# A bound on the scatters under way in a GNN layer: each tied scatter waits for the one three ahead of it

## The chip, the cores and the metric

The kernel runs on one core of a Trainium2 chip, in one launch. The metric is the device time of one execution in microseconds (us). Beside the timed runs there is one profiled execution, from which all durations below are taken.

## The reference, cut to what matters

A graph has 6250 nodes with 128 features each and 100,000 edges, which are sorted by their destination (`dst`) and have their sources (`src`) in no order. Each edge makes a message from its two nodes' features and its own 128 features; the messages are summed by source node.

```python
row, col = src, dst
h = jnp.concatenate([x[row], x[col], edge_attr], axis=-1) @ W + b
h = layernorm(h) * gamma + beta
msg = relu(h)
out = segment_sum(msg, row, num_segments=6250)
return layernorm(x + out)
```

## The kernel before, in words

**Tiles.** The edges are cut into 782 tiles of 128. Four tiles make a *slot* `q` (196 slots, `PT = 4`). The nodes are split into 50 blocks by `src % 50`, which are worked on as 25 pairs of blocks.

**First half of an edge's way (by slot).** For each slot, `edges` (L602) multiplies the edge features `eT` with the third part of the weights (L611) and adds the destination node's part, picked out of a small window of a table by a 0/1 matrix (L615). `evict` (L619) lets ScalarE copy the PSUM bank into one of eight buffers `hs_all[q % 8]` (L623), with the source's local number beside it (L624). The eviction of slot `q + 8` therefore needs the buffer of slot `q`. From there each tile is *scattered*: `scatters` (L630) issues one indirect DMA on the queue of POOL (GpSimd) for each tile (L641), 128 rows of 528 bytes, to the rows of a table in DRAM, `sorted_d[s]`, that DVE has worked out (`place_i`). So there are 782 scatters. After them the rows of each pair of blocks lie together.

**Second half (by pair of blocks).** The slots are in six splits (`SPLITS`, of 168, 168, 168, 120, 80 and 78 tiles, that is 42, 42, 42, 30, 20 and 19.5 slots). A split's table can be read when all its scatters have landed. `load_pair` (L711, DMA at L715, on SP's queue) loads a pair's rows into `hl`; six steps later `ones` (L730) lets DVE build a 0/1 matrix `ohe` from it (L733), and after that come the turned matrix (L745, L749), the source node's part (L755, L772), the norm (L781, L784, L790, L796), the sum by node (L805) and the addition to `acc` (L810). The last split's rows are loaded in `Unit.load` (L831, DVE's matrix at L838), after the last slot.

**The order.** PE, DVE, ScalarE and SP run in an order written out by hand (`tc.manual_schedule`, L973). POOL is not in that list: where its instructions stand is decided by the framework's scheduler, from what each depends on. The loop over slots (L1118) does a slot's edge work and, in between, steps of the pairs' work; a table of due times (`due`, L1095) says that the pairs of split `s` start `LAG = 5` slots after the split's last slot.

**What a scatter waits for.** Up to slot 12 and in slot 195 the scatters are *untied*: they wait for their data, their rows' numbers and a semaphore of the DMA queue. Between them they are *tied* (`TIE`, L627; `scatters(..., True)`, L1144): in each slot the scatters of the slot before are issued, and each of them waits, too, for one of that slot's matmuls, so that they are spread over the slot (L647). Eight semaphores are used in turn for the scatters' landing, and a scatter waits for the landing of the one eight ahead, which had the same semaphore. Scatters of one split do not wait for each other's rows (`declare_no_dep`, L648).

Of the kernel before, what the change touches and what calls it, by code (L numbers as in the profile page):

```python
# [84 lines left out]
def fast_path(ctx, tc, io, bad_d, found):  # L85
# [3 lines left out]
    nc = tc.nc  # L89
# [6 lines left out]
    written = mybir.DependencyInfo(mybir.DependencyClass.Sync, mybir.DependencyReason.DATA)  # L96
# [528 lines left out]
        waiting.extend((s, q, j) for j in range(m))  # L625

    TIE = (12, 195)  # L627
    waiting = []

    def scatters(n, tied):  # L630

        total, seen, at = sum(c for _, c in done), 0, []
        for i, c in done:
            seen += c
            while len(at) < n and seen * n >= (len(at) + 1) * total:
                at.append(i)
        done.clear()
        for k, (s, q, j) in enumerate(waiting[:n]):
            t = q * PT + j
            parts = P if t < TILES - 1 else LAST  # L640
            i = nc.gpsimd.indirect_dma_start(  # L641
                out=sorted_d[s][:, :],
                out_offset=bass.IndirectOffsetOnAxis(ap=place_i[:parts, t:t + 1], axis=0),
                in_=hs_all[q % HS][:parts, j, :], in_offset=None,
            )
            if tied:
                tc.add_manual_dep(i.ins, at[k].name, written, reason="rows behind products")  # L647
            tc.declare_no_dep(i.ins, group=f"scatter{s}", reason="rows of different edges")  # L648
            tc.add_to_no_dep_group(f"scatter{s}", i.ins)
            if q < EARLY:  # L650
                tc.declare_no_dep(i.ins, group="clear", reason="see check_early")
                tc.add_to_no_dep_group("early", i.ins)
        del waiting[:n]
# [461 lines left out]
    for s, (n_tiles, _, _, _) in enumerate(SPLITS):  # L1115
        p0, p1 = first_tile[s] // PT, -(-first_tile[s + 1] // PT)
        slots = p1 - p0
        for i in range(slots):  # L1118
# [19 lines left out]
            if not TIE[0] <= q < TIE[1]:  # L1138
                scatters(len(waiting), False)
# [3 lines left out]
            if TIE[0] < q < TIE[1]:  # L1143
                scatters(len(waiting) - PT, True)  # L1144
# [115 lines left out]
@with_exitstack  # L1260
def gnn_resnorm_kernel(ctx, tc, io):
    nc = tc.nc
    keep = ctx.enter_context(tc.tile_pool(name="keep", bufs=1))
    bad_t = keep.tile([1, 1], I32, name="bad_t")
    with ExitStack() as inner:
        found = []
        fast_path(inner, tc, io, bad_t, found)
    with tc.If(found[0] > 0, preferred_fallthrough_block=True, label="general"):
        with ExitStack() as inner:
            general_path(inner, tc, io)  # L1270
# [233 lines left out]
```

## Time and profile before

| what | value |
|---|---|
| median of 3 runs | 1369.37 us (1368.53, 1369.37, 1379.85) |
| the profiled execution's own time | 1380.69 us, of which the span from the first to the last instruction is 1378.9 us |
| granted TensorE clock in it | 0.857 of full speed |
| first and last start of a scatter (L641) in it | 19.9 us and 1274.6 us |
| first and last start of a pair's load (L715) in it | 297.5 us and 1278.7 us |
| first and last start of a unit's load (L831) in it | 1281.7 us and 1344.5 us |

The engines are named PE (TensorE), DVE (VectorE), ACT (ScalarE), POOL (GpSimd) and SP (SyncE, which issues most of the DMAs). In the profile, a group's line has the source line, the engine, the operation, what it writes and reads, the number of instructions, then the busy time and the mean of one in ns, and after the bar the idle time of that engine just before them with what ended most of it. The time of a scatter on POOL is that in which POOL writes the transfer's descriptors; its data move afterwards, on the DMA engines, in the queue that the profile calls `q0 software_dynamic`. All other transfers of the kernel are in `q1 hardware_dynamic`. A scatter of a full tile is 32 packets in q0: 16 of data and 16 that raise its semaphore.

### The profile page before, as it was taken

What the parts mean: (1) busy time and instruction counts of PE and PEld (TensorE: products, weight loads), DVE (VectorE), ACT (ScalarE), POOL (GpSimd) and SP (SyncE); (2) the same over time, 40 slices, a digit from 0 to 9 for tenths busy, and PEclk for the clock granted to TensorE, in tenths of its full rate; (3) what the DMA queues carried; (4) which work ended last, traced back from release to release, by engine and by line L of the source; (5) the groups of instructions that cost most, each with busy time, mean ns of one, the idle gap of its engine ahead of it and who ended that gap; (6) DMA issues with size and microseconds to landing.
All of it is one profiled execution on the core that took longest, in us unless ns stands there. A gap on an engine that the chain in (4) does not pass through costs nothing. (4 is left out here: it accounts for less than half of the span.)

```text
span 1378.9 us, 27543 instructions
## 1 busy us (share of the span) xinstructions
PE 975.2 (71%) x8886; PEld 870.3 (63%) x8886; DVE 855.0 (62%) x2376; ACT 773.5 (56%) x3118; POOL 798.9 (58%) x835
## 2 busy tenths in 40 slices
PE   7457464345767676778777677778778787876895
PEld 5445453334666665777676667777778776765674
DVE  8573434524465656556575657678688867554797
ACT  4223232112555655564565557676778788665796
POOL 3656666666566665666565666566555555556054
PEclk9768687666888989878888899999999999988898
DMA  7758586455666655556656555665667655543332
GB/s 223 236 168 255 171 241 204 142 154 155 184 199 210 199 158 163 178 157 198 207 171 200 172 184 178 208 208 187 190 193 227 183 181 171 170 140 100 112 122 72
DMA packets 128052, 247.22 MB, mean 179 GB/s; under 512 B 47005, under 2 KB 61231, under 8 KB 127897
## 3 DMA queue, kind: packets, MB, share of 16 engines
q1 hardware_dynamic: 101924, 191.92, 46.8%
q0 software_dynamic: 25104, 53.05, 11.0%
q8 instruction: 71, 1.16, 0.4%
q14 instruction: 83, 0.68, 0.2%
q10 hardware_dynamic: 870, 0.40, 0.1%
HBM read 155.49 MB, written 89.80 MB: 178 GB/s over the span
## 5 line engine op out<-in xcount | busy, mean ns | idle before, releaser
L641 POOL DMA_INDIRECT sorted<-hs,place_i x782 | 760.4, 972 | 498.1 <-issue 210.6
L772 PE MATMUL sel<-xa,ohn 128*128 128x128 bf16 x2550 | 214.3, 232 | 174.9 <-issue 78.5
L781 ACT ACTIVATE sq<-sel 128x128 f32<-128x128 f32 x850 | 224.2, 280 | 158.9 <-PE sel L772 58.2
L772 PEld LDWEIGHTS <-ohn 128*128 128x128 bf16 x2550 | 174.8, 104 | 204.4 <-issue 174.7
L611 PE MATMUL hp<-w,eT 128*128 128x128 f32 x1564 | 258.3, 314 | 51.2 <-issue 37.9
L611 PEld LDWEIGHTS hp<-w,eT 128*128 128x128 f32 x1564 | 234.3, 225 | 83.2 <-issue 59.3
L805 PE MATMUL pa<-msg,ohe 128*128 128x130 f32 x1700 | 259.2, 308 | 24.1 <-issue 14.9
L623 ACT COPY hs<-hp 128x512 f32<-128x512 f32 x196 | 114.2, 583 | 288.7 <-issue 97.7
L805 PEld LDWEIGHTS pa<-msg,ohe 128*128 128x128 f32 x1700 | 236.4, 217 | 32.2 <-issue 19.0
L796 DVE SCALAR_TENSOR_TENSOR msg<-sel,rstd,cut 128x128 f32<-128x128 f32 x850 | 240.7, 345 | 8.0
L781 ACT ACTIVATION_READ_ACCUMULATOR sq<-sel 128x1 f32 x850 | 178.8, 210 | 0.0
L810 DVE TENSOR_TENSOR acc<-acc,pa 128x260 f32<-128x260 f32 x125 | 53.0, 424 | 201.0 <-PE pa L805 57.9
L733 DVE TENSOR_TENSOR ohe<-hl,beside 128x1024 f32<-128x1024 f32 (+2 forms) x125 | 131.4, 1052 | 23.3 <-PE sel L772 14.6
L749 ACT COPY ohn<-tr 128x1024 bf16<-128x1024 bf16 (+2 forms) x125 | 109.5, 876 | 37.9 <-PE pa L805 14.7
L755 ACT COPY sel<-hl 128x512 f32<-128x512 f32 (+1 forms) x225 | 127.9, 569 | 1.8 <-DVE msg L796 1.0
L599 DVE TENSOR_SCALAR ohd<-db,part_w 128x512 bf16<-128x512 bf16 x192 | 69.7, 363 | 72.1 <-remote 50.9
L615 PE MATMUL hp<-win,ohd 126*128 126x128 bf16 x782 | 88.5, 236 | 17.4 <-issue 15.4
L790 DVE RECIPROCAL rstd<-std 128x4 f32<-128x4 f32 (+1 forms) x225 | 38.6, 171 | 96.7 <-ACT std L784 45.2
L615 PEld LDWEIGHTS <-ohd 126*128 126x128 bf16 x782 | 69.0, 108 | 25.2 <-issue 20.9
L745 PE MATMUL tr<-ident_h,ohe 128*128 128x128 bf16 x850 | 75.5, 230 | 11.1 <-issue 9.4
L784 ACT ACTIVATE std<-ss,eps 128x4 f32<-128x4 f32 (+1 forms) x225 | 66.9, 297 | 7.3
L745 PEld LDWEIGHTS <-ohe 128*128 128x128 bf16 x850 | 57.7, 103 | 14.3 <-issue 14.2
(198 smaller groups left out, 1043.4 us busy)
## 6 DMA issues: line engine op xcount, KB each, us to landing
eT<-in_eT SPq DMA_DIRECT2D x96, 512.0 KB
hl<-sorted SPq DMA_DIRECT2D x75, 528.0 KB
db<-drel_d SPq DMA_DIRECT2D x96, 256.0 KB
sorted<-empty SPq DMA_DIRECT2D x100, 198.0 KB
hl<-sorted SPq DMA_DIRECT2D x50, 264.0 KB
sorted<-hs,place_i POOLq DMA_INDIRECT x782
hl<-sorted SPq DMA_DIRECT2D x25, 396.0 KB
sorted<-empty SPq DMA_DIRECT2D x50, 132.0 KB
```

Of the source, the lines that this page charges most:

```text
L611: pe(nc.tensor.matmul(hp[:, j, :], eT[:, at], w[:, 2, :], start=j == 0, stop=False, skip_group_check=True), 4)
L615: pe(nc.tensor.matmul(hp[:, j, :], oh[:3 * WN, at], win[:3 * WN, :], start=False, stop=j == m - 1, skip_group_check=True))
L623: nc.scalar.copy(hs[:, :m, 0:D], hp[:, :m, :])
L641: i = nc.gpsimd.indirect_dma_start(out=sorted_d[s][:, :], out_offset=bass.IndirectOffsetOnAxis(ap=place_i[:parts, t:t + 1], axis=0), in_=h ...
L733: nc.vector.tensor_tensor(self.ohe[:, :k, :], self.hl[:, :k, D:D + 1].to_broadcast([P, k, P]), row_bc(iota_p, k), op=ALU.is_equal)
L745: pe(nc.tensor.transpose(tr[:, j, :], half[:, j0 + j, 1::2], ident_h))
L749: nc.scalar.copy(self.ohn[:, :self.k, :], self.tr[:, :self.k, :])
L755: nc.scalar.copy(self.sel[g][:, :m, :], self.hl[:, j0:j0 + m, 0:D])
L772: pe(nc.tensor.matmul(sel[:, j, :], self.ohn[:, j0 + j, :], xa[:, b, i * D:(i + 1) * D], start=False, stop=j == m - 1 and i == 2, skip_gro ...
L781: nc.scalar.activation(sq[:, j, :], self.sel[g][:, j, :], AF.Square, accum_out=ss[:, j:j + 1])
L796: nc.vector.scalar_tensor_tensor(self.msg[:, j0 + j, 0:D], self.sel[g][:, j, :], rstd[:, j:j + 1], cut, op0=ALU.mult, op1=ALU.max)
L805: pe(nc.tensor.matmul(self.pa[:, h, :], self.ohe[:, j, :], self.msg[:, j, :], start=(j == h), stop=(j == k - 2 + h)), 4)
```

## The change

Ahead of each tied scatter the changed kernel records an instruction without work on POOL (`nop`), named `hold`, and makes it depend on the completion of the scatter that was recorded three before (`issued[-FLIGHT]`). Nothing else is changed. The scatter itself is not made dependent on `hold`.

```diff
     TIE = (12, 195)
-    waiting = []
+    FLIGHT, EVERY = 3, 1
+    waiting, issued = [], []
 
     def scatters(n, tied):
...
         for k, (s, q, j) in enumerate(waiting[:n]):
             t = q * PT + j
             parts = P if t < TILES - 1 else LAST
+            if tied and len(issued) % EVERY == 0:
+                hold = nc.gpsimd.nop()
+                tc.add_manual_dep(hold.ins, issued[-FLIGHT].name, written,
+                                  reason="so many scatters under way")
             i = nc.gpsimd.indirect_dma_start(
                 out=sorted_d[s][:, :],
                 out_offset=bass.IndirectOffsetOnAxis(ap=place_i[:parts, t:t + 1], axis=0),
                 in_=hs_all[q % HS][:parts, j, :], in_offset=None,
             )
+            issued.append(i.ins)
             if tied:
                 tc.add_manual_dep(i.ins, at[k].name, written, reason="rows behind products")
```

## The prediction, made before the changed kernel ran

> **What bounds the kernel now.** I read the page first, then POOL's waits, because the change adds waits there and nowhere else: in the built program PE, DVE, ACT and SP keep the same instructions, order and waits.
>
> ```profile
> span 1378.9 us, 27543 instructions
> PE 975.2 (71%) x8886; PEld 870.3 (63%) x8886; DVE 855.0 (62%) x2376; ACT 773.5 (56%) x3118; POOL 798.9 (58%) x835
> ...
> q1 hardware_dynamic: 101924, 191.92, 46.8%
> q0 software_dynamic: 25104, 53.05, 11.0%
> ...
> L641 POOL DMA_INDIRECT sorted<-hs,place_i x782 | 760.4, 972 | 498.1 <-issue 210.6
> ```
> ```profile
> POOL sorted L641 <- issue: 210.6, 535, 3.4
> POOL sorted L641 <- PE pa L805: 64.6, 53, 3.0
> ...
> POOL sorted L641 <- DMA sorted<-hs,place_i: 0.9, 3, 0.3
> ```
>
> No engine is full. The hand-written slots set the pace, and POOL follows: it waits for PE's products, and for the landing of an earlier scatter hardly ever (0.9 us in all, 3 times; that wait is for the one eight ahead). Behind a held scatter stand only further scatters on POOL's queue, so one wait moves all that follow. A late scatter harms in two places only: the table of its split is read later, or its `hs` buffer is free later. So three things are needed: how long a landing takes, how many scatters back the new waits reach, and how far POOL may fall behind.
>
> **How long a landing takes.** Nothing on the page says it; POOL's timeline and q0's packets in small windows do.
>
> ```profile
> 653.99 0.97 POOL L641 DMA_INDIRECT sorted<-hs,place_i  x1 [1.22 <-PE pa L805]
> 655.26 0.97 POOL L641 DMA_INDIRECT sorted<-hs,place_i  x1 [0.30 <-issue]
> 657.08 0.97 POOL L641 DMA_INDIRECT sorted<-hs,place_i  x1 [0.85 <-PE hp L615]
> 658.35 0.97 POOL L641 DMA_INDIRECT sorted<-hs,place_i  x1 [0.30 <-issue]
> 659.63 0.97 POOL L641 DMA_INDIRECT sorted<-hs,place_i  x1 [0.30 <-issue]
> ...
> 665.13 0.97 POOL L641 DMA_INDIRECT sorted<-hs,place_i  x1 [1.98 <-ACT hs L624]
> ```
> Then q0 in 655.3 to 656.7 us and in 656.75 to 657.2, the queues in 657.2 to 660.5, and q0 in 657.2 to 661.3:
> ```profile
> q0 software_dynamic: 32, 0.07, 14.8%
> ```
> ```profile
> q0 software_dynamic: 32, 0.07, 47.9%
> ```
> ```profile
> q1 hardware_dynamic: 229, 0.70, 74.1%
> ```
> ```profile
> q0 software_dynamic: 59, 0.14, 11.3%
> ```
>
> A scatter has 32 packets. The first window holds those of 653.99, the second those of 655.26: it has landed by 657.2, **1.94 us** after its start. The scatter of 657.08 moves nothing up to 660.5, while q1 carries a table and an `eT` load, and is through only by about 661.2: **4.1 us**. The same operation takes twice as long in busy DMA, though the one ahead of it had all but landed.
>
> Then the step from a wait's end to the scatter's start. POOL's sequencer, in 656 to 662 us:
>
> ```profile
> L641 POOLq EVENT_SEMAPHORE  x5: 17/17/2977, 656.8 to 661.4; - x5
> ```
>
> The last wait begins at 661.4 and lasts 2.98, to 664.4; the scatter behind it starts at 665.13: **0.71 us**. A scatter that waits for the one d back thus costs, with the chain going round, (landing + 0.71)/d: 2.65/d in quiet DMA, 4.81/d in busy DMA, never below 1.28 (658.35 to 659.63).
>
> **How many back.** Nothing ties a hold to its scatter; POOL's order is the scheduler's, and in the built program the holds, turned into waits, run ahead of their scatters. Here `DMASW1` to `DMASW7` and `DMASW0` are the eight landing semaphores in their turn, and each scatter's own is among its waits (the one eight back):
>
> ```
> L646 DMACopy sorted_75<-hs_199,place_i 23040x132 [waits DMASW2_49,DMASW0_49,PE_49]
> L646 DMACopy sorted_75<-hs_199,place_i 23040x132 [waits DMASW3_49,DMASW1_49,PE_49]
> L646 DMACopy sorted_75<-hs_199,place_i 23040x132 [waits DMASW3_49,DMASW4_49,DMASW2_49,PE_49]
> ```
>
> The first waits for the scatter two back, the second too, the third (its own is 4) for the one just before it. Counted over the program, 538 scatters get an earlier wait; the nearest one reaches:
>
> | started (us) | scatters | 1 back | 2 back | 3 back | farther |
> |---|---|---|---|---|---|
> | 96 to 280 | 120 | 12 | 0 | 11 | 97 |
> | 280 to 544 | 168 | 11 | 20 | 49 | 88 |
> | 544 to 811 | 168 | 8 | 14 | 85 | 61 |
> | 811 to 1006 | 120 | 10 | 39 | 44 | 27 |
> | 1006 to 1142 | 80 | 9 | 49 | 6 | 16 |
> | 1142 to 1275 | 78 | 6 | 32 | 16 | 24 |
>
> So the change does not do what it says: in the last three stages most tied scatters run with one or two under way.
>
> **The sum.** POOL's windows for those stages (length, busy and count, clock, DMA share, GB/s):
>
> ```profile
> 96.20:280.40 184.20, 116.70 (x120) 0.73 0.67 201
> 280.40:544.10 263.70, 163.10 (x168) 0.83 0.57 176
> 544.10:811.20 267.10, 163.64 (x168) 0.83 0.59 182
> 811.20:1006.20 195.00, 116.75 (x120) 0.94 0.63 196
> 1006.20:1142.30 136.10, 77.57 (x80) 0.96 0.64 195
> 1142.30:1275.00 132.70, 75.15 (x78) 0.89 0.49 146
> ```
>
> I take the DMA share as the chance that a landing is a busy one (an estimate; the ends are all quiet and all busy). At 0.63 a scatter costs 0.63 x 4.81 + 0.37 x 2.65 = 4.01 (1 back), 2.01 (2 back), 0.63 x 1.60 + 0.37 x 1.28 = 1.48 (3 back), else 1.28.
>
> - 811 to 1006: 10 x 4.01 + 39 x 2.01 + 44 x 1.48 + 27 x 1.28 = 218 us of chain where the slots took 195.0: 23 late.
> - 1006 to 1142, share 0.64: 9 x 4.03 + 49 x 2.02 + 6 x 1.49 + 16 x 1.28 = 164.5 against 136.1: 28 more.
> - 1142 to 1275, share 0.49: 6 x 3.71 + 32 x 1.85 + 16 x 1.44 + 24 x 1.28 = 135.3 against 132.7: 3 more.
> - The first three stages by the same rule: 189.8, 265.9 and 262.0 against 184.2, 263.7 and 267.1; 5.6 + 2.2 - 5.1, so 3 late at 811.
>
> At its end POOL is 57 us late.
>
> **What hides it.** The last scatters before a split's read, the reads, and DVE's first use:
>
> ```profile
> 1141.09 0.97 POOL L641 DMA_INDIRECT sorted<-hs,place_i  x1 [0.30 <-issue]
> ```
> ```profile
> 1163.16 0.33 SPq L715 DMA_DIRECT2D hl<-sorted  x1
> ```
> ```profile
> 1174.49 0.68 DVE L733 TENSOR_TENSOR ohe<-hl,beside 128x512 f32<-128x512 f32 x1
> ```
> ```profile
> 1274.57 0.87 POOL L641 DMA_INDIRECT sorted<-hs,place_i  x1 [0.30 <-issue]
> ```
> ```profile
> 1281.71 0.32 SPq L831 DMA_DIRECT2D hl<-sorted  x1
> ```
> ```profile
> 1289.91 0.68 DVE L838 TENSOR_TENSOR ohe<-hl,beside 128x512 f32<-128x512 f32 x1
> ```
>
> q0's last packets and q1 in 1283 to 1284 us (the load of 1281.71; in 1284 to 1284.9 one packet is left):
>
> ```profile
> q0 software_dynamic: 32, 0.02, 10.6%
> ```
> ```profile
> q1 hardware_dynamic: 123, 0.23, 69.3%
> ```
>
> The first is the window 1276.0 to 1276.6, so the last scatter has landed by 1276.6. Slack at the end: 1281.71 - 1276.6 = 5.1, and 1289.91 - 1281.71 less 2.3 for the load = 5.9; together 11.0 us. For the split that ends with the scatter of 1141.09: 1163.16 - (1141.09 + 1.94) = 20.1, and 11.3 - 2.3 = 9.0; together 29 us, against 54 late. Behind that waiting load in SP's queue stand the next slots' `eT`, `db` and window loads, for PE. For the buffers:
>
> ```profile
> 1004.28 0.97 POOL L641 DMA_INDIRECT sorted<-hs,place_i  x1 [0.30 <-issue]
> ```
> ```profile
> 1045.79 0.59 ACT L623 COPY hs<-hp 128x512 f32<-128x512 f32 x1
> ```
>
> The scatter is slot 155's last, the copy slot 163's; 1045.79 - 1006.2 = 40 us, passed in the middle of the fifth stage. Slots stalled there move with POOL, so these stalls are not added: POOL stays late, and the end is 57 - 11 = 46 us later. A stalled kernel moves less data, and landings quicken: the last stage at a share of 0.40 costs 5 us less. I take 43: 1380.7 + 43 = 1424 for a profiled execution, 1369.4 + 43 = **1412 us** for the median, which is 11.3 below the profiled one.
>
> The bounds: all landings quiet leaves every stage under its slots (169 against 195, 117 against 136), so nothing; all busy makes 200 late, 189 at the end, before the thinning that such stalls bring. With landings of 2.9 us throughout the three late stages take about 197, 149 and 131 us, so 15 late at 1142 and 13 at the end, 2 more than the slack. The forecast's own range is 1383 to 1465.
>
> **The rivals.** (a) *Hidden: about 1369, 0.17.* If a held scatter meets quiet DMA more often than the share says, because a hold ends when a burst has passed, the costs are the quiet ones: 10 x 2.65 + 39 x 1.33 + 71 x 1.28 = 169 < 195, and no lag. It decides below some 2.9 us a landing. Against it stands 4.1 at 657.08. The Trainium skill, "DMA: Bandwidth & Descriptors", section "Anatomy of one DMA — SWDGE (gpsimd) path", has a DMA from GpSimd take a near-constant 2.0 us plus its bytes at 436 GB/s, an estimated 2.16 us for 67.6 KB; by that rule the fourth stage needs 10 x 2.87 + 39 x 1.44 + 71 x 1.28 = 176 us and the time stays 1369. The quiet scatter (1.94) agrees with it, the busy one does not.
>
> (b) *Faster: about 1354, 0.08.* PE loses time it has no visible reason to lose, most where DMA is full:
>
> ```profile
> L772 PE MATMUL sel<-xa,ohn 128*128 128x128 bf16 x2550 | 214.3, 232 | 174.9 <-issue 78.5
> ```
> ```profile
> 709.40:714.00 4.60, 1.58 (x9) 0.92 (x6) 4.56 (x8) 1.44 (x9) 2.91 (x3) 0.83 1.01 340
> 718.00:724.00 6.00, 6.00 (x66) 5.98 (x65) 4.86 (x20) 4.99 (x23) 4.13 (x5) 0.89 0.42 125
> ```
>
> With three scatters begun and DMA at 1.01 PE works 1.58 of 4.60 us, with DMA at 0.42 all of 6.00. Were q0's part of the packets' time (11.0 of 11.0 + 46.8, 19%) to blame for its part of those 78.5 us, holding scatters out of the bursts would give 15 us back: 1354. It needs POOL not to fall behind as well. The skill's "SBUF — State Buffer", section "Who interferes with whom", says that DMA and compute engines never contend; by it this case gives nothing.
>
> (c) *Much slower: 1465 to 1560, 0.05.* Landings busy almost throughout, with `hs` holding ACT from the second stage on.
>
> **The numbers.** The forecast has 0.70. A measurement of this kernel tells about 1% (14 us) from no change, since its runs spread over 11 us. Slower by over 1% (above 1383): the forecast's range and (c), 0.75. Within 1%: (a) and some of (b), 0.19. Faster: 0.06. The range 1366 to 1465 leaves out (b) and (c).
>
> **What would show it.** POOL's idle time ahead of L641 ended by a DMA grows from 0.9 us to well over 100. The scatter that is slot 175's last starts some 50 us after 1141, the load of its split right after its landing, and PE and DVE stand still around it. If slot 175 ends before 1160 and the time is above 1383, the sum is wrong and the cause is elsewhere; if POOL's waits for DMA are long but absorbed, (a) is right.

## The result and the profile after

The changed kernel takes **1521.19 us** (median of 4 runs, 1518.56 to 1537.03) where the kernel before took 1371.62 us beside it (1368.53 to 1379.85): a ratio of **1.1097, interval 1.1063 to 1.1132**. The forecast was 1412, the range 1366 to 1465. The direction was right, the loss 3.5 times what was foreseen (150 us against 43).

The page after, with the profiled execution's span (its own time is 1519.68 us), the engines' busy time, the queues and three groups:

```profile
span 1517.9 us, 27761 instructions
PE 1005.1 (66%) x8886; PEld 901.7 (59%) x8886; DVE 854.3 (56%) x2376; ACT 772.0 (51%) x3118; POOL 798.6 (53%) x835
...
q1 hardware_dynamic: 101924, 191.92, 41.1%
q0 software_dynamic: 25104, 53.05, 10.1%
...
L646 POOL DMA_INDIRECT sorted<-hs,place_i x782 | 760.1, 972 | 647.6 <-issue 203.4
...
L623 ACT COPY hs<-hp 128x512 f32<-128x512 f32 x196 | 114.3, 583 | 417.2 <-DMA sorted<-hs,place_i 198.1
```

POOL's busy time has not moved (760.4 to 760.1 us; the scatter's line is now L646). Its idle time ahead of the scatters has grown by 149.5 us, 498.1 to 647.6. No other engine works longer in a way that would explain 139 us of span: PE is 30 us busier at a lower granted clock (0.808 after 0.857), DVE and ACT are unchanged. The waits, first POOL's, then ACT's and SP's (total, times, longest):

```profile
POOL sorted L646 <- issue: 203.4, 487, 6.2
POOL sorted L646 <- DMA sorted<-hs,place_i: 154.1, 105, 5.2
```
```profile
ACT hs L623 <- DMA sorted<-hs,place_i: 198.1, 56, 9.3
```
```profile
SPq L721 <- DMA sorted<-hs,place_i: 67.4, 4, 21.1
```

POOL's waits for a scatter's landing went from 0.9 us to 154.1. ACT's idle time ahead of L623 went from 288.7 us to 417.2, of which 198.1 are put down to a buffer that a late scatter has not yet emptied, and SP waits up to 21.1 us at a time to read a split's table. So the lateness reaches the other engines by just the two ways that the prediction named.

The same six stages as in the prediction, cut at the starts of the same scatters (length, busy and count, clock, DMA share, GB/s):

```profile
94.40:301.30 206.90, 117.02 (x120) 0.72 0.60 184
301.30:592.30 291.00, 163.23 (x169) 0.78 0.52 165
592.30:877.10 284.80, 163.53 (x169) 0.79 0.53 168
877.10:1115.30 238.20, 116.47 (x121) 0.88 0.53 168
1115.30:1284.90 169.60, 77.53 (x80) 0.87 0.48 153
1284.90:1423.70 138.80, 74.67 (x78) 0.78 0.38 117
```

Every stage is longer than before, by 22.7, 27.3, 17.7, 43.2, 33.5 and 6.1 us. The scatters' times on POOL (shortest, median and longest in ns, first and last start), then the first loads of the last split on SP's queue, and DVE's first matrix from them:

```profile
L646 POOL DMA_INDIRECT sorted<-hs,place_i x782: 871/970/1130, 19.6 to 1423.7; - x196
```

```profile
1425.85 13.48 SPq L837 DMA_DIRECT2D hl<-sorted  x11
```
```profile
1428.47 0.69 DVE L844 TENSOR_TENSOR ohe<-hl,beside 128x512 f32<-128x512 f32 x1 [14.82 <-DMA hl<-sorted]
```

The last scatter starts 149 us later than before (1423.7 against 1274.6), and the profiled span ends 139 us later. The loads start 2.2 us after that scatter's start; before, they came 7.1 us after (1281.71 against 1274.57). DVE starts 2.6 us after the load; before, 8.2 us after (1289.91 against 1281.71). So the slack that the prediction counted at the end, 11.0 us, is used up, and it is about what is missing between 149 and 139.

### The profile page after: what moved, and what is told of

Its sections match the earlier page's. It is cut to its first block, busy times and chain, and to the rows that moved or that the text cites. A ratio compares the mean times of both kernels' runs of the same rounds, so it can differ in the third digit from the quotient of the medians.

```text
span 1517.9 us, 27761 instructions
## 1 busy us (share of the span) xinstructions
PE 1005.1 (66%) x8886; PEld 901.7 (59%) x8886; DVE 854.3 (56%) x2376; ACT 772.0 (51%) x3118; POOL 798.6 (53%) x835
## 3 DMA queue, kind: packets, MB, share of 16 engines
q1 hardware_dynamic: 101924, 191.92, 41.1%
## 5 line engine op out<-in xcount | busy, mean ns | idle before, releaser
L646 POOL DMA_INDIRECT sorted<-hs,place_i x782 | 760.1, 972 | 647.6 <-issue 203.4
L778 PE MATMUL sel<-xa,ohn 128*128 128x128 bf16 x2550 | 221.0, 241 | 222.6 <-ACT sel L761 144.1
L778 PEld LDWEIGHTS <-ohn 128*128 128x128 bf16 x2550 | 186.2, 109 | 244.2 <-issue 200.2
L623 ACT COPY hs<-hp 128x512 f32<-128x512 f32 x196 | 114.3, 583 | 417.2 <-DMA sorted<-hs,place_i 198.1
L811 PE MATMUL pa<-msg,ohe 128*128 128x130 f32 x1700 | 280.0, 319 | 53.7 <-issue 38.8
L611 PE MATMUL hp<-w,eT 128*128 128x128 f32 x1564 | 267.7, 321 | 63.4 <-ACT hs L623 45.0
L611 PEld LDWEIGHTS hp<-w,eT 128*128 128x128 f32 x1564 | 241.6, 231 | 100.6 <-ACT hs L623 46.7
L811 PEld LDWEIGHTS pa<-msg,ohe 128*128 128x128 f32 x1700 | 250.2, 226 | 69.6 <-issue 57.0
L751 PE MATMUL tr<-ident_h,ohe 128*128 128x128 bf16 x850 | 80.4, 236 | 29.6 <-issue 27.9
L751 PEld LDWEIGHTS <-ohe 128*128 128x128 bf16 x850 | 60.8, 107 | 32.2 <-issue 32.2
```

The source lines that it names most:

```text
L611: pe(nc.tensor.matmul(hp[:, j, :], eT[:, at], w[:, 2, :], start=j == 0, stop=False, skip_group_check=True), 4)
L623: nc.scalar.copy(hs[:, :m, 0:D], hp[:, :m, :])
L646: i = nc.gpsimd.indirect_dma_start(out=sorted_d[s][:, :], out_offset=bass.IndirectOffsetOnAxis(ap=place_i[:parts, t:t + 1], axis=0), in_=h ...
L751: pe(nc.tensor.transpose(tr[:, j, :], half[:, j0 + j, 1::2], ident_h))
L778: pe(nc.tensor.matmul(sel[:, j, :], self.ohn[:, j0 + j, :], xa[:, b, i * D:(i + 1) * D], start=False, stop=j == m - 1 and i == 2, skip_gro ...
L811: pe(nc.tensor.matmul(self.pa[:, h, :], self.ohe[:, j, :], self.msg[:, j, :], start=(j == h), stop=(j == k - 2 + h)), 4)
```

## The experiments

The record numbers the chips of the experiments (8 and 15), and there the kernel before took 1119 to 1126 us, not 1371; so each run is compared with the kernel before on its own chip. The record has no number for the chip of the first runs. It is called the first chip below; that it was another one, and that the chip makes the difference, is taken from the times alone.

**A larger number, same code.** Eight under way instead of three; the scheduler again decides where the holds stand. In the built program the nearest wait is one back for 55 scatters, two for 153, three for 195, four for 42 (with three: 56, 154, 211, 57).

```diff
-    FLIGHT, EVERY = 3, 1
+    FLIGHT, EVERY = 8, 1
```

> FLIGHT = 8 in place of 3, holds still placed by the scheduler. In the built program the nearest waits are almost the same as with 3: 55 scatters wait one back, 153 two back, 195 three back (56, 154, 211 in the change). Theory (POOL's chain of the waits as they stand in the program sets the time): 1505 to 1525 us, though eight may be under way by the text. Rival (the bound of three costs the time): eight back is the wait that was there before, so about 1371 us.

1500.57 us (4 runs), ratio 1.3396, interval 1.336 to 1.3431; a little under the range expected. The number in the source hardly matters: the time follows where the holds come to stand.

**Holds kept in place.** An order without a semaphore ties each hold behind the scatter before it, and the scatter behind its hold. Now the wait reaches exactly as many scatters back as the number says, for all tied scatters but one to three.

```diff
+    in_order = mybir.DependencyInfo(mybir.DependencyClass.NoSync, mybir.DependencyReason.DATA)
...
                 hold = nc.gpsimd.nop()
                 tc.add_manual_dep(hold.ins, issued[-FLIGHT].name, written,
                                   reason="so many scatters under way")
+                tc.add_manual_dep(hold.ins, issued[-1].name, in_order, reason="hold's place")
...
+            if tied:
+                tc.add_manual_dep(i.ins, hold.ins.name, in_order, reason="hold's place")
             issued.append(i.ins)
```

With `FLIGHT` 8, a wait that was there already:

> FLIGHT = 8, and each hold is kept in its place: order-only edges put it behind the scatter before its own and ahead of its own. Every wait is then eight back, as before the change; only the holds' instructions are added. Theory: 1366 to 1376 us, the time before. Rival (the added instructions on POOL's queue cost the time, not what they wait for): well above 1400 us.

1119.08 us (10 runs) against 1119.25, ratio 1.0001, interval 0.9991 to 1.001. (The 1366 to 1376 expected was the first chip's time.) The added instructions cost nothing; everything is the waits.

With `FLIGHT` 3, what the change says it does:

> FLIGHT = 3 with each hold kept in its place: 726 scatters wait exactly three back, none nearer. Theory: three back costs (landing + 0.74)/3, 1.0 to 1.6 us a scatter, at or under the slots' pace of 1.54 to 1.77, so 1366 to 1385 us. Rival (a true bound of three is as dear as the change): about 1521 us. Second rival (fewer scatters under way relieve PE): under 1358 us.

1368.24 us, ratio 1.2214, interval 1.2182 to 1.2246. The time lies where it was expected, but by luck: it was to be the slots' pace, hardly slower than before, and before took 1119 us here. A true bound of three costs 22%.

With `FLIGHT` 2:

> FLIGHT = 2 with each hold kept in its place: 725 scatters wait exactly two back. Theory: (3.3 + 0.74)/2 = 2.0 to 2.2 us a scatter, above the slots' pace everywhere, POOL bound from the first stage on: 1640 to 1720 us. Rival (landings get quicker when fewer are under way, down to 2.1 us): (2.1 + 0.74)/2 = 1.4 us a scatter, about 1371 us.

1662.58 us (2 runs), ratio 1.4855, interval 1.4812 to 1.4898.

**Which chip.** The kernel before and the changed one once more, on a chip of the faster kind, each with a profile:

> The kernel before, unchanged, profiled again beside the others: the kernels of the first call shared runs of it of 1119 us, where it had taken 1369 to 1372 us until then. Theory: where it takes 1119 us, POOL is the bound already (1.28 us a scatter throughout) and the unexplained idle time of PE (78.5 us ahead of L772 in the first profile) is gone; where it takes about 1370 us, POOL's pace is 1.54 to 1.77 us again. Rival: the same waits in both and another cause, the granted clock for instance.

> The change, unchanged, beside the kernel before on the same chip. Theory (POOL's chain of holds sets its time whatever the rest does): 1490 to 1530 us, also where the kernel before takes 1119 us, so a ratio of 1.11 or of about 1.34 with the chip. Rival (the holds add a fixed part to the slots' time): the ratio stays 1.11, 1240 us beside 1119.

Before: 1125.57 in its profile, 1122.51 the median. After: 1503.35 (4 runs), ratio 1.3401, interval 1.3347 to 1.3455. So the changed kernel takes nearly the same on both chips, and the kernel before does not. The kernel before on the faster chip, the page:

```profile
PE 880.2 (78%) x8886; PEld 810.2 (72%) x8886; DVE 849.3 (76%) x2376; ACT 766.8 (68%) x3118; POOL 799.0 (71%) x835
...
POOL 3677777777777777777777777777777766675254
...
q1 hardware_dynamic: 101924, 191.92, 55.7%
...
L641 POOL DMA_INDIRECT sorted<-hs,place_i x782 | 760.6, 973 | 254.3 <-issue 103.2
```

The waits, here and then in the first chip's profile of the same kernel:

```profile
POOL sorted L641 <- issue: 103.2, 338, 0.4
...
PE sel L772 <- ACT sel L755: 106.2, 80, 6.7
...
PE tr L745 <- issue: 7.2, 1, 7.2
```
```profile
PE sel L772 <- issue: 78.5, 110, 2.4
PE sel L772 <- ACT sel L755: 74.8, 44, 8.1
PE hp L611 <- issue: 37.9, 23, 11.8
PE sel L407 <- issue: 31.8, 7, 9.2
```

On the faster chip POOL starts a scatter every 1.28 us without a pause (idle steps of 0.3 us, the even 7s in the slices), and that sets the pace: POOL has nothing to spare, so each microsecond of waiting shows in the time. On the first chip PE is idle for 404 us of the span, on the faster one for 244. The slots wait with PE, and POOL can catch up: the change loses 150 us on the first chip and 381 on the other, so that room hid some 230 us. (That PE's idle time is the room is argued; no run on the first chip tests it.)

The rows put 148 us of PE's idle time on the first chip down to "issue", at three lines, and on the faster chip no such row has more than 7.2 us. That doesn't show idle time without a cause. The first two traces hold 6700 and 10,164 changes of semaphores by DMAs; those of the same two kernels on the faster chip hold 21,710 and 22,181. Where the end of a wait was not recorded, the wait may stand as "issue".

The faster chip's traces show the waits best. POOL's waits for a landing there, in the kernel before and in the changed one:

```profile
POOL sorted L641 <- DMA sorted<-hs,place_i: 34.7, 114, 0.3
```
```profile
POOL sorted L646 <- DMA sorted<-hs,place_i: 200.3, 180, 5.3
```

A wait for several semaphores is put down to one of them, so these rows are the least it can be. The trace also has the times at which the scatters' semaphores changed, and the built program has the scatters that each one waits for. The 728 tied scatters of the changed kernel take 381 us more than 1.28 us each (the kernel before: 9 us), which is about the whole loss. 375 of these stand ahead of scatters that start within 1.15 us of the last landing that they wait for.

**More buffers.** If lateness only did harm by way of the eight `hs` buffers, two more would mend some of it.

```diff
-    HS = 8
+    HS = 10
```

> The change with ten hs buffers in place of eight. Theory (POOL's chain is the bound; the buffers only pass its lateness on): within 1% of the change. Rival (the buffers' number is what holds ACT and PE back, as its waits for L623 suggest): two slots more of cover, 15 us faster or more.

1519.99 us (2 runs), ratio to the kernel before 1.3542, interval 1.3498 to 1.3585, a little above the change itself (1.3401), with the same waits in the built program. The buffers pass POOL's lateness on to ACT; they don't cause it.

**The price of depth.** Exactly four back, as a further point:

> FLIGHT = 4 with each hold kept in its place, 727 scatters wait exactly four back. Theory, with landings of 2.3 (quiet) and 5 to 5.4 us (busy), half of each: 1.28 and (5.2 + 0.74)/4 = 1.49, so 1.38 us a scatter: 1190 to 1230 us where the kernel before takes 1119, and no change where it takes about 1370. Rival (a bound on the scatters under way costs in itself): near 1368, the time with three.

1226.31 us, ratio 1.0917, interval 1.0871 to 1.0964. The stretch from the 168th to the 504th scatter, 336 of them, in the kernel before and with four, three and two back (length, busy and count, clock, DMA share, GB/s):

```profile
237.00:666.00 429.00, 326.70 (x336) 0.90 0.71 226
```
```profile
257.70:732.20 474.50, 326.15 (x337) 0.88 0.65 205
```
```profile
284.00:828.70 544.70, 325.80 (x336) 0.81 0.57 178
```
```profile
328.30:1010.60 682.30, 325.25 (x337) 0.75 0.45 142
```

Divided by 336 that is 1.28, 1.41, 1.62 and 2.03 us per scatter. The prediction's rule, at these shares of DMA, gives 1.28 for eight and four back, 1.46 for three and 1.81 for two: too little at each depth that waits.

What is too small in it can be read from the same stretch. Call a landing the time from a scatter's start on POOL to the last recorded change of its semaphore; at least 15.5 of the 16 steps of a scatter are recorded here on average. Nearly all scatters that waited for a landing start 0.74 us after it. The mean landing is 4.16 us with eight back, 3.83 with four, 3.51 with three and 3.14 with two; the quiet ones, up to 2.6 us, take 2.3 us, the others 4.1 to 4.5 on average. The table has the time per scatter, first with each scatter's own landing in the rule, (landing + 0.74)/d but at least 1.28, then with the same landings followed through in order: each scatter starts 1.28 us after the one before it, or 0.74 us after the landing that it waits for, whichever is later.

| back | by the rule | followed in order | measured |
|---|---|---|---|
| 4 | 1.35 | 1.40 | 1.41 |
| 3 | 1.52 | 1.60 | 1.62 |
| 2 | 1.94 | 2.01 | 2.03 |

So the landings explain the pace, but not by the rule. It shares each landing out among d scatters. POOL's queue is in order: a long landing holds its scatter and all that stand behind it, and the quick landings behind it don't give that back.

**Early or late.** The prediction had 3 of its 57 us of lateness in the first three stages. Holds only up to slot 125, then only from slot 126:

```diff
-            if tied and len(issued) % EVERY == 0:
+            if tied and q < 126 and len(issued) % EVERY == 0:
```

> The change's holds only ahead of the scatters issued in slots 13 to 125, which are the first three stages (nearest waits in the built program: 31 reach one back, 34 two, 145 three, 56 four). Theory (POOL's own chain sets the time from the first stage on, nothing in these stages hides it where the kernel before takes about 1120 us): each class costs its measured pace less 1.28 us, 31 x 2.76 + 34 x 0.89 + 145 x 0.40 + 56 x 0.15 = 182 us, so about 1300 us. Rival (the prediction's: these stages have room, 3 us late in all): 1120 to 1140. If the chip is one on which the kernel before takes about 1370 us, the later stages have time to catch up and the theory gives 1370 to 1400.

```diff
-            if tied and len(issued) % EVERY == 0:
+            if tied and q >= 126 and len(issued) % EVERY == 0:
```

> The change's holds only ahead of the scatters issued from slot 126 on, the last three stages (nearest waits: 25 reach one back, 120 two, 66 three). Theory: 25 x 2.76 + 120 x 0.89 + 66 x 0.40 = 202 us over a kernel before of 1120, so about 1320 us, and the two halves' losses add up to the whole change's 381. Rival (nearly all of the loss is made in the late stages): 1480 to 1500. If the kernel before takes about 1370 us here, the theory gives 1440 to 1460.

1311.53 us (ratio 1.1696, interval 1.1673 to 1.1719) and 1308.35 us (1.1672, 1.164 to 1.1703), the kernel before 1120.89; about 1300 and 1320 had been expected. The halves lose 190.6 and 187.5 us, together 378, where the whole change lost 381. POOL's scatters before and after the 504th, first in the early, then in the late version:

```profile
83.00:853.70 770.70, 441.96 (x457) 0.78 0.56 175
853.70:1216.20 362.50, 268.74 (x277) 0.98 0.70 224
```
```profile
81.80:663.00 581.20, 441.57 (x456) 0.87 0.74 233
663.00:1209.50 546.50, 267.75 (x277) 0.83 0.46 149
```

Where there are no holds POOL runs at 1.27 to 1.31 us a scatter, where there are, at 1.69 and 1.97. Nothing is given back later and nothing is shared between the halves.

**Does a landing depend on other transfers?** Each pair of slots loads its `eT` once more, into a buffer that nobody reads; with exactly two back, and in the kernel before as a control.

```diff
             edge_feats(q)
+        w1 = min(g * PT * P, (TILES - t0) * P)
+        spare = edge.tile([P, DG * PT * P], F32, name="spare", bufs=1)
+        nc.sync.dma_start(spare[:, :w1], io["eT"][:, t0 * P:t0 * P + w1])
```

> Exactly two back for every tied scatter, as in the run that took 1663 us, and besides each pair of slots loads its eT once more into a buffer that nobody reads: 98 transfers of 512 KB more on SP's queue, 241 MB instead of 192 MB in q1. Theory (a landing takes 2.3 us in quiet DMA and about 5 in a burst of q1): a quarter more of the time is burst, the mean landing goes from 3.1 to about 3.35 us, half of that per scatter, so some 85 us more: 1710 to 1790 us. Rival (a landing is a fixed time that other transfers don't change): 1650 to 1680.

> The kernel before with the same 98 additional loads. It is the control for the run with two back: here the only wait is for the scatter eight ahead, 8 x 1.28 = 10.2 us earlier, so that longer landings cost nothing. Theory: within 25 us of the kernel before on the same chip (1120 to 1145 where that takes 1120), so that what the loads cost in the run with two back is due to the landings. Rival (the additional loads cost time by themselves, for instance because PE's operands come later): the same 60 us or more in both.

1757.11 us (2 runs) where two back without the loads took 1662.58, and 1128.24 us (2 runs; ratio to the kernel before 1.0063, interval 1.0039 to 1.0087). The same loads cost 94 us there and 7 here. The control's bulk queue (191.92 MB without the loads):

```profile
q1 hardware_dynamic: 116036, 243.18, 66.2%
```

The stretch of 336 scatters, two back with the loads, then the control:

```profile
347.50:1076.40 728.90, 325.57 (x337) 0.75 0.49 164
```
```profile
242.70:671.20 428.50, 326.06 (x337) 0.91 0.83 278
```

With the loads two back needs 2.17 us a scatter instead of 2.03. The mean landing in the stretch is 3.41 us instead of 3.14, and half of that difference is the difference in pace. In the control DMA is at 0.83, the fullest of these stretches, and the mean landing is 5.04 us, yet POOL's pace is 1.28: eight under way cover even these. That is what the scatters under way are for, and what the change takes from them.

## Why the prediction was right in direction and wrong in size

**Right: what the change does.** The holds run ahead of their scatters and most waits reach one to three back; the run with eight in the source, which lost the same, shows that it is their place and not their number. That POOL's waits for landings make the time is the mechanism, and each depth has its pace. Two of the signs named ahead came: POOL's idle time ended by a DMA went from 0.9 to 154.1 us, and a split's load came right behind its last landing. Slot 175's last scatter, the load, and DVE's first matrix from it:

```profile
1283.67 0.97 POOL L646 DMA_INDIRECT sorted<-hs,place_i  x1 [0.78 <-PE sel L778]
```
```profile
1286.05 0.82 SPq L721 DMA_DIRECT2D hl<-sorted  x2
```
```profile
1288.92 0.69 DVE L739 TENSOR_TENSOR ohe<-hl,beside 128x512 f32<-128x512 f32 x1 [5.18 <-DMA hl<-sorted]
```

The load starts 2.4 us after the scatter, and DVE stands 5.18 us for it. But that scatter starts 143 us later than before (1283.67 against 1141.09), where about 50 had been named.

**Wrong: the sum of the stages, by the price of a wait.** The step that failed is "A scatter that waits for the one d back thus costs, with the chain going round, (landing + 0.71)/d", used for each scatter by itself. The price holds when all of the d scatters under way land equally late. Here long and quick landings are mixed, and a scatter that reaches two or three back stands among others that reach farther. An instance from the changed kernel, on POOL's timeline:

```profile
888.73 0.97 POOL L646 DMA_INDIRECT sorted<-hs,place_i  x1 [0.30 <-issue]
890.01 0.97 POOL L646 DMA_INDIRECT sorted<-hs,place_i  x1 [0.30 <-issue]
891.28 0.97 POOL L646 DMA_INDIRECT sorted<-hs,place_i  x1 [0.30 <-issue]
895.02 0.97 POOL L646 DMA_INDIRECT sorted<-hs,place_i  x1 [2.77 <-DMA sorted<-hs,place_i]
896.29 0.97 POOL L646 DMA_INDIRECT sorted<-hs,place_i  x1 [0.31 <-issue]
```

The scatter of 895.02 reaches three back. The one of 888.73 lands at 894.28, 5.55 us after its start. By the rule that costs (5.55 + 0.71)/3 = 2.09 us; it cost 3.74, as the two in between had taken 1.28 and 1.27, and the next one takes 1.27.

What the classes cost in the changed kernel, as the mean time from one scatter's start to the next, worked out from the 782 starts of the timeline and the nearest wait of each in the built program; in the last column the same on the faster chip:

| nearest wait | scatters | priced at | measured | missing, us | measured, faster chip |
|---|---|---|---|---|---|
| 1 back | 56 | 3.96 | 4.04 | 4 | 4.15 |
| 2 back | 154 | 1.98 | 2.17 | 29 | 2.18 |
| 3 back | 211 | 1.47 | 1.68 | 44 | 1.59 |
| 4 back | 57 | 1.28 | 1.43 | 8 | 1.53 |
| 5 back and farther | 250 | 1.28 | 1.30 | 6 | 1.29 |

The 56 at one back, where nothing is divided, were priced right. The miss is 0.2 us on each of 365 scatters at two and three back. With the few others it makes 91 us, and the sum was 57 where the last scatter was 149 late: 92 short.

The landings were not the miss. On the faster chip, where the changed kernel's trace is nearly whole (15.9 of 16 steps), 58% of them take over 2.6 us, 4.2 on average, close to the prediction's share and its 4.1. (Its two samples were read from packets. At the semaphore the quiet landings in the first chip's traces take 2.1 us, and the one of 657.08 at least 4.6.) With these landings in place of 1.94 and 4.1, and 0.74 for 0.71, the rule gives 1233 us for the 728 tied scatters, no more than the 1235 that the prediction's six stages add up to. Followed in order, the same landings give 1294, and 1313 were measured. So the division is 60 of the 80 us missing there; the rest fits a longer step from landing to start, since with 0.85 in place of 0.74 the landings in order give 1316. In the first chip's trace, with 6.6 of 16 steps recorded, the same three numbers are 1221, 1276 and 1323: the division is 56 of 102, and what makes the other 47 is open, since landings there may be later than recorded.

**Wrong: the first three stages.** Most of what was missing was there (3 us foreseen, 67.7 measured, that is 65 of 92), and 145 of the 211 scatters at three back stand in them. The prediction read 262.0 against 267.1 us as a stage with room, and subtracted it. The halves show the loss of the early holds by themselves, 191 us where POOL has no room.

**Right, but no help: "A stalled kernel moves less data, and landings quicken".** The share of DMA did fall (0.57 to 0.52 in the second stage, 0.63 to 0.53 in the fourth). On the faster chip the mean landing in the stretch of 336 scatters fell from 4.16 us before the change to 3.46 after it. The run with more loads shows that other transfers lengthen landings; how much fewer scatters in the queue shorten them, no run separates. The eight under way had covered the longer landings for nothing; the change makes the shorter ones cost time.

**Half right: the buffers.** That ACT stalls for them was said, as a thing of the fifth stage; of the 198.1 us, 63.7 lie in the first stage already. The run with ten buffers shows that this costs nothing of its own, as assumed in the sum.

**Right: what hides it, on that chip.** 11.0 us were to be hidden at the end; 149 us of lateness became 139 of span in the profiled executions. The medians lie 150 apart, and the kernel before spreads over 11 us, so the times alone don't show it.

**The rivals.** (a) Hidden: fallen. The Trainium skill, "DMA: Bandwidth & Descriptors", section "Anatomy of one DMA — SWDGE (gpsimd) path", with its near-constant 2.0 us, holds for the quiet landings (2.3 us here) and not for the others: other transfers alone moved the mean landing from 3.14 to 3.41 us and the time by 94. (b) Faster: fallen on both chips; PE's idle time ahead of L778 put down to "issue" fell from 78.5 to 57.9 us, but PE waited more for ACT (74.8 us before):

```profile
PE sel L778 <- ACT sel L761: 144.1, 61, 7.1
PE sel L778 <- issue: 57.9, 65, 4.8
```

The runs with more loads give no sign that DMA slows PE's work: with 51 MB more in q1 PE was busy for 1023.9 us, without them for 1023.8, two back in both. PE's idle time can't tell there, as POOL sets the pace. The busy time agrees with the Trainium skill, "SBUF — State Buffer", section "Who interferes with whom", by which DMA and compute engines never contend. (c) Much slower, 1465 to 1560: its range holds the time, and half of its reason came true, the buffers holding ACT from early on. Landings busy throughout did not come: with 58% over 2.6 us on the faster chip, four in ten stay quiet.

**What stays open.** Why the kernel before took 1371 us on the first chip: PE, DVE and ACT stood still there for longer, the rows for it rest on a trace with a third of the DMAs' semaphore changes, and in no later run did the kernel before take that long. Exactly one back was not tried. No version that was run is faster than the kernel before.

## What to carry to other kernels

A bound on the transfers under way costs at least (landing + the step from the semaphore to the next issue) / depth wherever that exceeds the issue interval. Where long and quick landings are mixed it costs more than the mean of that: follow the landings through in order, since in a queue that is in order a long one is paid and a quick one gives nothing back. Where a bound is written as an instruction of its own, see in the built program where that instruction stands. Slack that one profile shows in other engines may be gone elsewhere, and then the same change costs its full price. Before idle time is called idle without a reason, count whether the trace holds the semaphore changes that it should.

## What the runs showed of the hardware

An unchanged kernel took 1371 us in the first runs and 1119 to 1126 on two other chips, with the same instructions and the same busy time of POOL (760.4 and 760.6 us for the scatters), but with PE busy for 975.2 against 880.2 us, idle for 404 against 244, and a granted clock of 0.857 against 0.913. The cause is open.

A scatter's landing is no fixed time: 2.3 us for the quiet ones, 4.1 to 4.5 on average for the others, and 4.8 and more for a tenth even with two under way. With eight under way even the fullest long stretch (a DMA share of 0.83, a mean landing of 5.04 us) left POOL's pace at 1.28 us, and the change's instructions by themselves cost nothing (a ratio of 1.0001 with one ahead of each tied scatter). With the holds kept in place, a scatter that waits for a landing starts 0.74 us after its semaphore's last change.
